# One-core decoder layer with a 32-expert mixture on Trainium2: experts' results written to six places per token and summed at the end

## The chip, the core and the metric

The kernel runs on one core of one Trainium2 chip. The metric is device time in microseconds (us). Before the change the median of three runs is 601.46 us (599.84 to 603.62). One further execution was profiled; it took 602.7 us.

## What is computed

2,048 tokens of width 256 (16 sequences of 128, float32) pass three residual sub-layers, each behind a layer norm:

```python
x = x + latent_attention(layernorm(x))     # causal, width 32, rotary
x = x + cross_attention(layernorm(x), ctx) # 32 heads of width 8, 8 key groups, causal
x = x + experts(layernorm(x))              # 32 experts, inner width 96
```

The expert layer decides what the change touches:

```python
probs = softmax(x @ gate.T)                       # 32 per token
top, idx = top_k(probs, 8)
cum = cumsum(top / sum(top))
num_keep = min(sum(cum < 0.8) + 1, 8)             # at least one expert
share = top * (arange(8) < num_keep); share /= sum(share)
out[token] = sum over kept e of share * (silu(g_e(x)) * u_e(x)) @ down_e.T
```

A token can keep up to seven experts, as the seven largest of eight hold at least 7/8 of their sum, more than 0.8. In the data drawn here no token keeps more than six, and 6,801 of the 16,384 token-expert pairs are kept.

## The kernel before

**Blocks and steps.** Everything goes by blocks of P = 128 tokens, one sequence each, B = 16 of them. The instruction order is written out by hand: a loop over steps t (L1063 and after), four steps to a block, issues in each step the score products of a block's cross attention (step, L616: products of keys and queries, a row maximum by VectorE at L656, a second product and the exponential by ScalarE at L661, four score buffers in flight), and squeezes in between pieces of other work, as Python generators that are advanced by one piece per half step: weigh (the product with the values, o_ps, L669), divide, project (L697 to L712, result into xres, which holds all tokens' residual), route, the queries, keys and latent attention of the next group of four blocks, and the early tiles.

**Route** (L714 to L844). For one block or a pair of blocks: layer norm (statistics with one GpSimd operation at L368, the normalisation on VectorE at L373), two transposes (L396), gate product l_ps (L734), the eight largest, exponentials, cumulative sums by three shifted additions (L764), the list of kept experts (kept, L781), a counting product r_ps (L785) with a triangular matrix that ranks each token among those of its expert, the destination rows di (L811), and the shares written into the row tile (L818). Two blocks are routed together, as one set of instructions, except blocks 8, 9 and 12 to 15, which are routed alone: 11 routes. A row has 292 numbers: 256 of data, the token number, and 32 shares. Seven indirect DMAs per block (L825, on GpSimd's queue, the k-th kept expert of every token of the block) scatter the rows to xs in DRAM, one region of 2,048 rows per expert. They are put in a list, waiting, and taken from it two or four to a step.

**Early tiles.** Once the first ten blocks (NEARLY) are counted, expert regions have up to 24 (NF) full tiles of 128 rows whose rows are all sent. These run beside the rest of the attention and behind it, one slot per step at first and two in the last steps and behind them (first_slot, L948 to L985). Tile i passes four slots: its rows are loaded by SP's queue (ext, L935), its two transposes on TensorE (L968) copied by ScalarE (L978); the gate and up product and silu (L167 to L170); a transpose back (L960); the down product with a per-tile weight load ewd (L941 to L944, 96 KB, SP's queue), and the scaling by the share out of the row tile (ScalarE, L984). Then add_rows (L155) issues an accumulating indirect DMA on GpSimd's queue (L157), which adds the tile's 128 result rows of 256 numbers to one of three accumulators acc in DRAM, taken in turn; the index it reads is the column of token numbers in the row tile ext, of which there are six buffers.

**Load of the down weights.** All 32 experts' down weights, 3.1 MB, are loaded by load_down (L846) in four DMAs on SP's queue in step last + 3, when the attention's memory is released.

**Zeros.** From step 4 on SP issues three of a list of bulk DMAs per step: zeros to the padding of xs, zeros to the three accumulators (48 DMAs of 128 KB), then the experts' gate and up weights.

**Late tiles.** After the last block's route the lists of remaining tiles are built from the counts. Then 32 tiles (one per expert, its last rows) and further ones in chunks of four, each under a branch, run one after the other: rows by SP's queue six tiles ahead (L1223), transposes (L1230), copy (L1232), gate and up product (L1239), silu, transpose back (L1256), down product (L1269), share (L1273) and add_rows. In this data there are 23 full early tiles and 52 late ones, the rounding to four included. For an expert's last tile a predicated copy on VectorE (L1261) masks the token numbers of rows that another tile has.

**The sum at the end** (L1323 to L1340). For two blocks at a time SP loads the three accumulators' rows (24 DMAs of 256 KB), VectorE adds them to xres (L1333, L1335), and the output goes out on ScalarE's queue.

## Time and profile before

| | us |
|---|---|
| median of three runs | 601.46 |
| profiled execution | 602.7 |
| its span in the profile | 600.8 |
| granted TensorE clock, mean | 0.869 |
| attention and what runs beside it, until about | 357 |
| early tiles behind the attention, until the first late row load | 459 |
| late tiles and the landing of their last result, until | 572 |
| sum at the end | 29 |

| engine | busy us | share of the span |
|---|---|---|
| TensorE (PE) | 454.9 | 76% |
| VectorE (DVE) | 350.2 | 58% |
| GpSimd (POOL) | 284.6 | 47% |
| ScalarE (ACT) | 181.0 | 30% |

PE is TensorE's products, PEld its weight loads, which overlap them; SP is the engine whose queue issues most loads. L12 is line 12 of the kernel. In the rows by line, "out<-in" names the destination and the source, "x24" is the number of instructions, then come busy time in us and the mean of one in ns, then the idle time of the engine just ahead of these instructions and what ended it. In the table of waits, "a <- b" says that a waited for b, then the total in us, how often, and the longest. In the rows of the timeline the start and the length in us come first and, in brackets, how long the instruction waited and for what. The share "DMA" is the mean busy share of the core's sixteen DMA engines; GB/s is what they moved. A share over the whole span mixes the stages above.

### The profile page before, as it was taken

The numbers are of one execution on the slowest core, as the hardware profiler recorded it, in microseconds if no ns is written. First come the engines' busy times: TensorE is split into PE (matmuls) and PEld (weight loads), VectorE is DVE, ScalarE is ACT, GpSimd is POOL, SyncE is SP. The second block draws the span as 40 slices with busy tenths as digits, with TensorE's granted clock in tenths as the row PEclk, the third lists the DMA queues.
The fourth block names the chain that finished last, engine by engine and source line by source line (L and its number), as shares of the span: only waits on it lengthen the run. The fifth ranks groups of instructions, "written<-read, shape, count | busy, mean of one in ns | idle before, by whom it ended". The sixth has DMA issues, their size and how long they took to land.

```text
span 600.8 us, 12118 instructions
## 1 busy us (share of the span) xinstructions
PE 454.9 (76%) x4148; PEld 321.1 (53%) x4148; DVE 350.2 (58%) x1222; ACT 181.0 (30%) x450; POOL 284.6 (47%) x292
## 2 busy tenths in 40 slices
PE   4969788986998998988889996445662999988500
PEld 3736475654756665666666655344541666666300
DVE  3464476585676766677757764313440677665456
ACT  1121134333343343523325453112210333332200
POOL 5611230020462473627540478736574688887600
PEclk9978789999899898977889898867775999999955
DMA  8201275705704349301112145864633356567788
GB/s 269 70 1 37 54 172 142 211 1 142 247 28 141 109 123 234 119 16 51 37 35 82 37 94 135 215 149 98 131 58 99 79 103 123 103 107 140 124 272 288
DMA packets 64423, 70.25 MB, mean 117 GB/s; under 512 B 12722, under 2 KB 58808, under 8 KB 64064
## 3 DMA queue, kind: packets, MB, share of 16 engines
q1 hardware_dynamic: 45488, 51.66, 30.3%
q0 software_dynamic: 16320, 14.97, 14.1%
q10 hardware_dynamic: 2544, 2.75, 1.3%
q8 instruction: 35, 0.57, 0.4%
q14 instruction: 36, 0.29, 0.2%
HBM read 38.97 MB, written 42.13 MB: 135 GB/s over the span
## 4 chain that ended last, share of the span: by engine, by line
PE 43%; DVE 21%; DMA 18%; issue 6%; ACT 6%; POOL 3%; SPq 1%; POOLq 0%; DVEq 0%; ACTq 0%
PE s_ps L636 6%; DMA ewd<-in_w_dn_t 5%; DVE nmz L656 4%; PE o_ps L669 4%; PE s_ps L642 4%; DMA part<-acc 4%; DMA acc<-y,xt 4%; ACT xT L1232 2%; PE h_ps L1256 2%; PE q_ps L578 2%; PE s_ps L649 2%; DMA q<-qd 2%; PE egx_ps L968 2%; DVE ga L169 2%; DVE h L170 2%
## 5 line engine op out<-in xcount | busy, mean ns | idle before, releaser
L825 POOL DMA_INDIRECT xs<-row,di x112 | 110.8, 990 | 36.8 <-issue 30.2
L656 DVE TENSOR_REDUCE nmz<-s_ps 128x4 f32<-128x512 f32 x128 | 82.4, 686 | 61.1 <-PE s_ps L649 58.2
L661 ACT ACTIVATE pt<-s_ps 128x512 f32<-128x512 f32 x128 | 69.5, 595 | 104.1 <-PE s_ps L649 99.8
L636 PE MATMUL s_ps<-k,q 32*128 32x128 f32 x1024 | 88.2, 307 | 0.5 <-DVE xres L506 0.5
L642 PE MATMUL s_ps<-q8m,k 32*128 32x512 f32 x256 | 79.7, 709 | 5.5 <-DVE q8m L611 2.6
L636 PEld LDWEIGHTS s_ps<-k,q 32*128 32x128 f32 x1024 | 74.9, 207 | 3.5 <-issue 1.8
L157 POOL DMA_INDIRECT acc<-y,slot x32 | 49.4, 1542 | 19.9 <-DVE y L1273 10.4
L1239 PE MATMUL g<-wgu,xT 128*128 128x192 f32 (+1 forms) x212 | 53.3, 335 | 3.8 <-issue 3.8
L157 POOL DMA_INDIRECT acc<-ey,ext x24 | 37.8, 1575 | 26.3 <-ACT ey L984 17.4
L1232 ACT COPY xT<-x_ps 128x256 f32<-128x256 f32 x55 | 20.5, 372 | 87.2 <-PE x_ps L1230 67.3
L958 PE MATMUL eyh_ps<-ewd,ehT 96*128 96x256 f32 x48 | 19.6, 497 | 33.2 <-DMA ewd<-in_w_dn_t 31.8
L1239 PEld LDWEIGHTS g<-wgu,xT 128*128 128x128 f32 x212 | 36.8, 196 | 8.1 <-ACT th L167 4.5
L669 PE MATMUL o_ps<-pt,va 128*32 128x512 f32 x256 | 38.1, 670 | 1.9 <-DVE xres L712 1.9
L642 PEld LDWEIGHTS s_ps<-q8m,k 32*128 32x128 f32 x256 | 22.1, 203 | 30.4 <-issue 19.5
L169 DVE SCALAR_TENSOR_TENSOR ga<-th,g 128x96 f32<-128x96 f32 x53 | 13.5, 254 | 41.1 <-ACT th L167 27.4
L1269 PE MATMUL y_ps<-wdn,hT 96*128 96x256 f32 (+1 forms) x104 | 35.9, 427 | 0.1
L157 POOL DMA_INDIRECT acc<-y,xt x20 | 30.8, 1542 | 9.6 <-DVE hT L1258 6.9
L675 ACT ACTIVATE ot<-o_ps,tab 128x512 f32<-128x512 f32 x32 | 22.1, 690 | 31.4 <-PE o_ps L669 27.6
L1230 PE MATMUL x_ps<-tab,xt 128*128 128x128 f32 x110 | 22.1, 285 | 11.4 <-DMA xt<-xs 11.3
L958 PEld LDWEIGHTS eyh_ps<-ewd,ehT 96*128 96x128 f32 x48 | 9.4, 232 | 37.0 <-issue 31.2
L368 POOL TENSOR_TENSOR rs_f<-ve_f,mhalf 128x1 f32<-128x1 f32 (+1 forms) x11 | 7.5, 686 | 44.6 <-DVE ve_f L366 44.6
L978 ACT COPY exT<-egx_ps 128x256 f32<-128x256 f32 x24 | 8.9, 373 | 64.0 <-PE egx_ps L968 64.0
(261 smaller groups left out, 884.6 us busy)
## 6 DMA issues: line engine op xcount, KB each, us to landing
xt<-xs SPq DMA_DIRECT2D x58, 146.0 KB
acc<-zero SPq DMA_DIRECT2D x48, 128.0 KB
wgu<-in_w_gu_t SPq DMA_DIRECT2D x32, 192.0 KB
part<-acc SPq DMA_DIRECT2D x24, 256.0 KB
xs<-zero SPq DMA_DIRECT2D x33, 146.0 KB
ext<-xs SPq DMA_DIRECT2D x24, 146.0 KB
ewd<-in_w_dn_t SPq DMA_DIRECT2D x24, 96.0 KB
ct<-in_ctx_t SPq DMA_DIRECT2D x4, 512.0 KB
```

Source lines behind the costliest of these rows:

```text
L157: nc.gpsimd.indirect_dma_start(out=acc[i % NACC], out_offset=bass.IndirectOffsetOnAxis(ap=tokens, axis=0), in_=y, in_offset=None, bounds_c ...
L169: nc.vector.scalar_tensor_tensor(a, th, 1.0, g, ALU.add, ALU.mult)
L636: nc.tensor.matmul(s_ps[:, i, :], lhsT=q8[g % 2][rows, i, tok], rhs=k8[g % 2][h][rows, tok], start=(i == 0), stop=True, skip_group_check=True,
L642: nc.tensor.matmul(s_ps, lhsT=k8[g % 2][h][rows, tok], rhs=q8ms[b][rows, :, :], start=True, stop=True, skip_group_check=True,)
L656: nc.vector.tensor_reduce(nmz[b % 2][:, :, 32 * r + h], s_ps, AX.X, ALU.max, negate=True)
L661: nc.scalar.activation(pt, s_ps, AF.Exp)
L669: nc.tensor.matmul(o_ps[32 * r : 32 * r + 32, :, :], lhsT=vaug[b % NVA][:, 4 * h + r, :], rhs=pts.pop((b, h, r)), start=True, stop=True,)
L825: sent = nc.gpsimd.indirect_dma_start(out=xs, out_offset=bass.IndirectOffsetOnAxis(ap=di[:, j, k : k + 1], axis=0), in_=row[:, j, :], in_o ...
L958: nc.tensor.matmul(y_ps, lhsT=down["hT"], rhs=down["wd"], start=True, stop=True)
L1232: nc.scalar.copy(v["xT"], x_ps)
L1239: nc.tensor.matmul(v["g"], lhsT=v["xT"][:, c, :], rhs=wgu_flat[:, bass.ds(v["e"] * W2 + c * NE * W2, W2)], start=(c == 0), stop=(c == KC - 1),
L1269: nc.tensor.matmul(y_ps, lhsT=hT, rhs=wdn[:, bass.ds(v["e"] * D, D)], start=True, stop=True)
```

## The change

It has five parts.

1. **Places.** A DRAM buffer ys has six rows per token and a section with one more row per token for a seventh. Each result row is written to a place of its own by a plain indirect DMA, with no order among these DMAs; an index beyond the buffer is dropped. The place of a token's result for an expert is six times the token number plus the number of its kept experts ahead of this one, a prefix sum over 32 columns: nine more VectorE operations in each route, with a running maximum that tells whether any token keeps a seventh. Row tiles are 320 wide: 256 of data and 32 pairs of share and place. In an early tile's slot ScalarE copies the pair out of the row tile and VectorE turns the place into an index; in a late tile one VectorE operation does so, masked where it is an expert's last tile. The row tiles of early tiles have five buffers instead of six. Zeros are written to all of ys (16 DMAs of 768 KB and 4 of 512 KB) in place of the accumulators.
2. **The sum at the end** loads one block's 128 x 6 rows with one DMA (768 KB, 6 KB contiguous per partition, eight buffers in the memory of the gate and up weights); VectorE adds the first half to the second and GpSimd two of the three rows that are left, VectorE adds the third and GpSimd's sum to the residual; an output DMA follows per block. A branch ahead of it adds the seventh section if a token has one.
3. **Routes.** All blocks are routed alone, 16 routes; the list of waiting sends is kept by blocks, and its thresholds change with it.
4. **Counting later.** While the attention runs, the counting product is issued half a step later; the prefix sum and what follows it stand in a further piece of the generator.
5. **The down weights' four DMAs** are issued on ScalarE's queue.

```diff
-RW = 292
-R_TOK, R_SHARE = D, D + 1
+RW = D + 2 * NE
+R_PAIR = D
+KEPT = 6
+NOWHERE = 16384
...
+    ys = dram.tile([(KEPT + 1) * B * P, D], F32, tag="ys", name="ys")
...
-    def add_rows(i, y, tokens):
-        nc.gpsimd.indirect_dma_start(
-            out=acc[i % NACC],
-            out_offset=bass.IndirectOffsetOnAxis(ap=tokens, axis=0),
-            in_=y, in_offset=None, bounds_check=B * P - 1, oob_is_err=False,
-            compute_op=ALU.add,
+    def place_rows(y, place):
+        sent = nc.gpsimd.indirect_dma_start(
+            out=ys, out_offset=bass.IndirectOffsetOnAxis(ap=place, axis=0),
+            in_=y, in_offset=None, bounds_check=(KEPT + 1) * B * P - 1, oob_is_err=False,
         )
+        tc.declare_no_dep(sent.ins, group="placed", reason="places are distinct")
+        tc.add_to_no_dep_group("placed", sent.ins)
...
-            g, pair = b0, b0 // 2
-            if b0 % 2 == 0:
-                while waiting and waiting[0][0] < pair - 2:
-                    waiting.pop(0)[1]()
-                rows[pair] = work.tile([P, 2, RW], F32, tag="row", bufs=3, name=f"row_{g}")
-                nc.gpsimd.memset(rows[pair][:, :, R_SHARE + NE :], 0.0)
-                nc.gpsimd.tensor_copy(
-                    rows[pair][:, :, R_TOK].bitcast(I32), num[:, b0 : b0 + 2]
-                )
-            row = rows[pair][:, b0 % 2 : b0 % 2 + nb, :]
+            g = b0
+            while waiting and waiting[0][0] < b0 - 3:
+                waiting.pop(0)[1]()
+            row = work.tile([P, nb, RW], F32, tag="row", bufs=4, name=f"row_{g}")
+            pairs = row[:, :, R_PAIR:].rearrange("p j (e i) -> p j e i", i=2)
...
+            nc.vector.tensor_tensor(seventh, seventh, act[:, 0, 6:7], ALU.max)
...
             yield
+            if dense[0]:
+                yield
             r_ps = mm([P, nb, NE], f"r_ps_{g}")
...
+            yield
+            pre = [t[:, 0:nb, :] for t in pres]
+            nc.vector.tensor_copy(pre[0][:, :, 17:], kept[:, :, 0 : NE - 1])
+            for k in range(5):
+                c, d = pre[k % 2], 1 << k
+                nc.vector.tensor_tensor(
+                    pre[1 - k % 2][:, :, 16:], c[:, :, 16:], c[:, :, 16 - d : 16 - d + NE], ALU.add
+                )
+            nc.vector.tensor_scalar(
+                pre[0][:, 0, 16:], pre[1][:, 0, 16:], float(KEPT),
+                tab[:, C_SEVENTH + b0 : C_SEVENTH + b0 + 1], ALU.is_ge, ALU.mult,
+            )
+            nc.vector.scalar_tensor_tensor(
+                pairs[:, 0, :, 1], pre[1][:, 0, 16:], tab[:, C_PLACE + b0 : C_PLACE + b0 + 1],
+                pre[0][:, 0, 16:], ALU.add, ALU.add,
+            )
             nc.vector.tensor_tensor(kept, kept, ex[:, :, 0:NE], ALU.mult)
             sk = small.tile([P, nb], F32, tag="sk", name=f"sk_{g}")
...
-                row[:, :, R_SHARE : R_SHARE + NE], kept, 0.5,
+                pairs[:, :, :, 0], kept, 0.5,
...
-                    waiting.append((pair, lambda j=j, k=k: send(j, k)))
+                    waiting.append((b0, lambda j=j, k=k: send(j, k)))
...
-                nc.sync.dma_start(
+                nc.scalar.dma_start(
...
-        bulk += [(a[b * P : (b + 1) * P, :], zero[:, 0:D]) for a in acc for b in range(B)]
+        for b in range(B):
+            r = b * P * KEPT
+            bulk.append(
+                (
+                    ys[r : r + P * KEPT, :].rearrange("(p k) d -> p k d", k=KEPT),
+                    zero[:, 0:D].unsqueeze(1).to_broadcast([P, KEPT, D]),
+                )
+            )
...
+        for b in range(0, B, 4):
+            r = (KEPT * B + b) * P
+            bulk.append(
+                (
+                    ys[r : r + 4 * P, :].rearrange("(k p) d -> p k d", p=P),
+                    zero[:, 0:D].unsqueeze(1).to_broadcast([P, 4, D]),
+                )
+            )
...
-        alone = (NEARLY - 2, NEARLY - 1, *range(B - 4, B))
-        routed = {b: (b - 1, 2) for b in range(1, B, 2)}
-        routed.update({b: (b, 1) for b in alone})
+        waiting, turn, count, counted = [], [0], [0], []
+        routed = {b: (b, 1) for b in range(B)}
...
-            v["xt"] = ebuf.tile([P, RW], F32, tag="ext", bufs=SOON + 4, name=f"ext_{k}")
+            v["xt"] = ebuf.tile([P, RW], F32, tag="ext", bufs=SOON + 3, name=f"ext_{k}")
...
+                pair = ebuf.tile([P, 2], F32, tag="epair", bufs=5, name=f"epair_{i}")
+                nc.scalar.copy(pair, turn_["xt"][:, bass.ds(2 * e_act + R_PAIR, 2)])
+                turn_["place"] = ebuf.tile([P, 1], I32, tag="eplace", bufs=6, name=f"eplace_{i}")
+                nc.vector.tensor_scalar(
+                    turn_["place"], pair[:, 1:2], float(NOWHERE), None, ALU.add
+                )
+                turn_["share"] = pair[:, 0:1]
...
-                nc.scalar.mul(y, y_ps, down["xt"][:, bass.ds(e_act + R_SHARE, 1)])
-                add_rows(i - 3, y, down["xt"][:, R_TOK : R_TOK + 1].bitcast(I32))
+                nc.scalar.mul(y, y_ps, down["share"])
+                place_rows(y, down["place"])
...
-            if t >= last or waiting and 4 * NEARLY < t and waiting[0][0] < NEARLY // 2:
+            if t >= last or waiting and 4 * NEARLY < t and waiting[0][0] < NEARLY:
...
+        pair = v["xt"][:, bass.ds(2 * e_dve + R_PAIR, 2)]
+        place = hbuf.tile([P, 1], I32, tag="place", bufs=4, name=f"place_{i}")
         if i < NE:
-            nc.vector.copy_predicated(slot[:, i : i + 1], valid[:, i : i + 1], tokens)
-            tokens = slot[:, i : i + 1]
+            nc.vector.tensor_scalar(
+                place, pair[:, 1:2], valid[:, i : i + 1], float(NOWHERE), ALU.mult, ALU.add
+            )
+        else:
+            nc.vector.tensor_scalar(place, pair[:, 1:2], float(NOWHERE), None, ALU.add)
...
-        nc.vector.tensor_scalar(
-            y, y_ps, v["xt"][:, bass.ds(e_dve + R_SHARE, 1)], None, ALU.mult
-        )
-        add_rows(NF + i, y, tokens)
+        nc.vector.tensor_scalar(y, y_ps, pair[:, 0:1], None, ALU.mult)
+        place_rows(y, place)
...
-    PB = 2
-    for b in range(0, B, PB):
-        part = hbuf.tile([P, NACC, PB, D], F32, tag="part", bufs=3, name=f"part_{b}")
-        for k in range(NACC):
-            nc.sync.dma_start(
-                out=part[:, k, :, :],
-                in_=acc[k][b * P : (b + PB) * P, :].rearrange("(b p) d -> p b d", p=P),
-            )
-        xg = xres[:, b : b + PB, :]
-        for k in range(NACC - 1):
-            nc.vector.tensor_tensor(xg, xg, part[:, k, :, :], ALU.add)
-        for j in range(PB):
-            nc.vector.scalar_tensor_tensor(
-                xg[:, j, :], xg[:, j, :], some[:, b + j : b + j + 1], part[:, NACC - 1, j, :],
-                ALU.mult, ALU.add,
-            )
-        nc.scalar.dma_start(
-            out=out[b * P : (b + PB) * P, :].rearrange("(b p) d -> p b d", p=P), in_=xg
+    with tc.If(nc.values_load(sevenths[0:1, 0:1], min_val=0, max_val=B * P) > 0):
+        for b in range(B):
+            part = hbuf.tile([P, D], F32, tag="part7", bufs=2, name=f"part7_{b}")
+            r = (KEPT * B + b) * P
+            nc.sync.dma_start(out=part, in_=ys[r : r + P, :])
+            nc.vector.tensor_tensor(xres[:, b, :], xres[:, b, :], part, ALU.add)
+    parts = wgu_flat.rearrange("p (n k d) -> p n k d", n=8, d=D)
+    for b in range(B):
+        part = parts[:, b % 8, :, :]
+        nc.sync.dma_start(
+            out=part,
+            in_=ys[b * P * KEPT : (b + 1) * P * KEPT, :].rearrange("(p k) d -> p k d", k=KEPT),
         )
+        half = hbuf.tile([P, KEPT // 2, D], F32, tag="half", bufs=3, name=f"half_{b}")
+        nc.vector.tensor_tensor(half, part[:, 0:3, :], part[:, 3:6, :], ALU.add)
+        both_b = hbuf.tile([P, D], F32, tag="both", name=f"both_{b}")
+        nc.gpsimd.tensor_tensor(both_b, half[:, 0, :], half[:, 1, :], ALU.add)
+        xb = xres[:, b, :]
+        nc.vector.scalar_tensor_tensor(
+            xb, xb, some[:, b : b + 1], half[:, 2, :], ALU.mult, ALU.add
+        )
+        nc.vector.tensor_tensor(xb, xb, both_b, ALU.add)
+        nc.scalar.dma_start(out=out[b * P : (b + 1) * P, :], in_=xb)
```

## The prediction

> **What bounds the kernel now.** I read the span in stretches first, then who waits for whom in each stretch, then single instructions. The table of stretches (start:end, length, busy time of each engine, granted TensorE clock, DMA share, GB/s):
>
> ```profile
> core 0: us, PE busy (x) PEld busy (x) DVE busy (x) ACT busy (x) POOL busy (x), PEclk, DMA share, GB/s
> 250.00:357.00 107.00, 94.73 (x1148) 67.85 (x1146) 74.28 (x283) 43.57 (x96) 49.70 (x59) 0.87 0.18 50
> 357.00:442.00 85.00, 49.66 (x250) 37.91 (x246) 30.79 (x154) 21.80 (x69) 54.46 (x49) 0.78 0.61 135
> 442.00:459.00 17.00, 5.15 (x26) 3.89 (x26) 4.93 (x26) 0.45 (x1) 12.80 (x12) 0.52 0.24 47
> 459.00:572.00 113.00, 93.94 (x478) 67.54 (x478) 66.78 (x242) 33.80 (x108) 80.20 (x52) 0.95 0.60 114
> 572.00:601.00 29.00, 0.00 (x0) 0.00 (x0) 17.74 (x32) 0.00 (x0) 0.00 (x0) 0.50 0.86 290
> ```
>
> Four regimes. Up to 357 us TensorE is nearly full. From 357 to 459 no compute engine is: 102 us for 20 slots of early tiles. From 459 the 52 late tiles run one after the other, TensorE bound. The last 29 us are transfer alone, 6.29 MB of sums in and 2.10 MB out. The waits inside 357 to 460 (waiter <- awaited: us in total, times, longest), of TensorE and then of SP's queue:
>
> ```profile
> PE eyh_ps L958 <- DMA ewd<-in_w_dn_t: 31.8, 8, 14.5
> ...
> SPq L935 <- DMA acc<-ey,ext: 55.1, 13, 13.6
> SPq L1223 <- DMA xs<-row,di: 12.6, 1, 12.6
> ```
>
> TensorE stands 31.8 us for weights of an early tile; SP stands 55.1 us at the row load ahead of them in its order (L935), because the row buffer is still read by an accumulating DMA: its token numbers are the index. The 14.5 is one wait, where that weight load lies behind the four down-weight loads of 379 us. Then SP waits 12.6 us for GpSimd's last sends.
>
> **The change, part by part**, against the profiled execution's 602.7 us.
>
> Places instead of sums. GpSimd's price today, per DMA:
>
> ```profile
> L825 POOL DMA_INDIRECT xs<-row,di x112 | 110.8, 990 | 36.8 <-issue 30.2 <-DVE row L818 3.0 <-DVE xn_a L373 1.1
> ...
> L157 POOL DMA_INDIRECT acc<-ey,ext x24 | 37.8, 1575 | 26.3 <-ACT ey L984 17.4 <-ACT xnt_f L400 3.6 <-issue 2.5
> ```
>
> A plain scatter takes 0.99 us, an accumulating one 1.57; back to back each adds 0.30 of idle. A place is a plain scatter of 1,024 B rows, so between 0.97 and 1.57; I take 0.99, the row of the same kind. From the first early result on, GpSimd has 40 sends and 24 results today: 40 x 1.29 + 24 x 1.87 = 96.5 us. In the built order of the change it has 31 sends and 24 places there, since blocks routed alone hand over their sends earlier: 55 x 1.29 = 71 us. The place and share are copied out of the row tile (one ScalarE copy, one VectorE operation per early tile), so the load at L935 no longer waits for a result to land.
>
> From 357 to 459 us. Of the 31.8, I keep 5 for the down weights, which still move 3.1 MB through the same sixteen engines while row and weight loads go on: -26.8. ScalarE issues the four down-weight loads, 1.8 us on SP today, and 24 small copies: +2. SP's 12.6 shrinks to what the last block's own sends need: its last counting product (L785) is followed by about 4.5 us of VectorE and 9 scatters of 1.3, 16 us, where today the last send starts 20.4 after it (436.7 to 457.2): -4. Together some **-28**. The counting starts a step later, so one slot of 2.9 us (neighbours start at 409.86 and 412.76) moves behind that product, where TensorE and the late lists end after 13 us and the sends after 18: it is hidden there, and 2 us fall out of the attention. Bounds of the 28: -35 if the weights cost nothing beside the rest and the sends wait for nothing, -13 if the 14.5 stay and half of the 4 is won. Late next: VectorE's and ScalarE's part of a slot, or GpSimd's 71 us, which from 346 end no earlier than 417; my 431 for the first late row load lies behind both.
>
> Here a rule speaks against the change. The wait of 14.5 us began when SP had issued 3.1 MB just ahead. The Trainium skill, "DMA: Bandwidth & Descriptors", "Issuing engines are not separate DMA queues", says that a second issuing engine saves issue time alone, as all transfers run on the same engines. By it the sum would be 9.5 higher, 604.0. The same page, "Queues, rings and completion order", lets each engine take turns between queues packet by packet, which a load behind others in one queue has not; no row of this trace shows the two queues busy with loads together.
>
> Routing alone, prefix sums, counting later (up to 357 us). TensorE's first score products of a step show the pace. Block 8's route, alone, falls into 272.7 to 289.6, 16.9 us for a block. One pair's route falls into the two blocks from 222.8 to 255.1, 16.1 each with 1.8 of key and value products: 14.3 without. So a lone route costs up to 2.6 us more per block. Ten blocks lose their partner; the first six lie before 250 us, where TensorE is 88 to 90% busy and has the next groups' products to do meanwhile, so I let half show there: 6 x 1.3 + 4 x 2.6 = +18. The counting product (L785) waits today:
>
> ```profile
> 279.29 0.64 PE L785 MATMUL r_ps<-kept,tab 128*128 128x32 f32 x2 [1.41 <-DVE kept L781]
> ...
> 280.29 1.94 PE L669 MATMUL o_ps<-pt,va 128*32 128x512 f32 x8
> ```
>
> After the wait the product L669 takes 1.94 us; without one, at 270.93, 1.07. Moved behind that product, the count waits some 0.5 and the product runs at 1.07: -1.7 for each of the 14 blocks routed before 357 us, -24. Against that stand nine more VectorE operations per block at a spacing of 0.2 (L764 takes 0.175), 1.8 us. They are queued ahead of the next block's normalisation (L373), for which TensorE's transposes (L396) wait: in the lone block's rows TensorE could take these at some 285.2 at the new pace, while VectorE, after the score reductions (1.3), the nine and the shares (2.4) and the normalisation (0.6), is there at 286.8. So the 1.7 is lost again; half in the eight blocks with cover, 8 x 0.9 + 6 x 1.8 = +18. Together 18 - 24 + 18 = **+12**, and **-2** for the slot that leaves. Bounds of the 12: -6 with the nine hidden, +27 with all of the split's 26 and all of the nine's 25 shown.
>
> Zeros and wider rows. 14.7 MB of zeros instead of 6.3 is 23 us of all engines at the 362 GB/s seen from 584 to 597, in a stretch (107 to 250) with shares of 0.40 and 0.59, so about 74 us free. The queue's next reader, the third group's queries, has 60 us until its first step. **0**, bound +3. Rows of 1,280 for 1,168 B: within that.
>
> Late tiles. From the first transpose to the last result, 465.7 to 565.2, 52 tiles take 99.5 us; at the steady 1.83 they would take 95.2. The surplus holds the stall from 545.7 to 553.9, a row load that waits 5.42 us for an accumulating DMA. It goes; GpSimd's 1.85 per tile falls to 1.3, but TensorE stays at 1.83. **-3**, from -4.3 to +3.4, the latter if 20 added operations of 0.17 were all exposed; VectorE is 59% busy here, which hides them.
>
> Last landing and branch. Issue to first sum load is 5.7 us today (566.4 to 572.1); a plain scatter is issued in 0.99 and lands in a median of 2.7 after its issue: -2. The branch over the seventh place, not taken unless a token keeps seven, costs every engine a load and a jump: +1. **-1**, from -2 to +2.
>
> The sum at the end. 12.58 MB in and 2.10 out, 14.68 for 8.39. Packets of 1,024 B have a median of 46 ns and of 4,096 B 159 ns, 22.3 and 25.8 B/ns on each of 16 engines; a place row is 6,144 B. Two measured stretches bound it:
>
> ```profile
> 382.00:396.00 14.00, 1.30 (x10) 1.04 (x8) 1.47 (x6) 1.15 (x4) 8.93 (x11) 0.72 1.04 268
> 584.00:597.00 13.00, 0.00 (x0) 0.00 (x0) 10.52 (x19) 0.00 (x0) 0.00 (x0) 0.50 1.04 362
> ```
>
> The first is the down weights in rows of up to 10,240 B, the second today's sums. At 362 GB/s the stage grows from 23.2 to 40.6, +17.4; with loads at 268 and outputs at 362 to 52.7, +29.5; at the 412 that 25.8 B/ns would be, to 35.6, +12.4. I take 385, between the rates of 1 and 4 KB: 38.1, **+15**. VectorE's three additions a block (1.0 + 0.48 + 0.4 by the 0.69 and 0.48 of L1333 and L1335) and GpSimd's one (0.7, a quarter of 2.36 and some fixed part) fit in the 2.4 that a block's bytes take.
>
> The Trainium skill, "SBUF — State Buffer", "Who interferes with whom", says that VectorE with two SBUF inputs and GpSimd reading SBUF block each other. No row shows that here; run one after the other, the same rows give an estimate of 2.6 for the 2.4 of a block and put the sum 3 higher.
>
> Sum: 12 - 2 - 28 + 0 - 3 - 1 + 15 = -7, so 595.7 for an execution like the profiled one. That one lies 1.2 above the median of 601.46; **594.5** beside the median.
>
> **Rivals.** First, the place rows load slowly. Large rows ran at 268 GB/s in the one stretch that has them; against it, that source has rows 32 KB apart on 96 partitions, and places are contiguous. Price 29.5 - 15 = 14.5: **609**, slower than before. The sign turns where the last stage grows by over 22, and 1% is passed below some 277 GB/s of loads.
>
> Second, VectorE becomes the bound of the attention. For it: 74.3 of 107 us busy already, and four score buffers tie it to TensorE; against it, up to 250 us there is cover. With all of split and nine shown, +27 for +12: **609.5**. It decides where a block's VectorE work passes TensorE's, both 15 to 17 us by the rows above.
>
> Third, the stretch behind the attention doesn't shrink as told: the second queue does nothing for the weights, or the row load meets another late reader. -13 for -28: **609.5**.
>
> Fourth, the nine operations hide wholly, -6 for +12: **576.5**.
>
> **Chances.** The forecast 0.50, its own range 586 to 602; slow rows 0.13; VectorE 0.15; the small shrink 0.10; all hidden 0.12. About 1% (6 us) is what a measurement can tell from none. Of the forecast's half, 0.32 lies below 595.4; with the hidden case, faster 0.44. The slow cases scatter round 609, and two of them together go beyond 620: of their 0.38, 0.30 lies above 607.5, with 0.02 of the forecast slower 0.32; same 0.24. With a tenth left out at either end: 577 to 616.
>
> **What would show it.** Right: TensorE's wait for early weights falls from 31.8 to under 10 us, SP's for an early result's landing is gone, the first late row load lies 15 to 30 us nearer to the last score product, GpSimd's places take 0.99, late tiles stay at 1.83, and the last stage takes some 44 us at about 385 GB/s. Wrong: a block of attention over 18.5 us with VectorE without idle time; a rate of the last stage below 330 GB/s; a wait of over 10 us behind the down weights.

## The result and the profile after

The change makes the kernel slower: 653.49 us (median of 4 runs, 647.14 to 659.46) for 601.52, a ratio of 1.079 (95% interval 1.073 to 1.086). The ratio compares the fast executions alone, without the one of 659.46. The prediction was 594.5, at most 616. The profiled execution took 654.26 us, its span 652.5 for 600.8.

Where the time went, from the first and last instructions of the stages in the two profiles (us):

| stage | before | after | difference | predicted |
|---|---|---|---|---|
| start to the last score product | 357.9 | 408.4 | +50.5 | +10 |
| from there to the first late row load | 101.3 | 81.7 | -19.6 | -28 |
| late tiles, to the issue of the last result | 107.1 | 106.5 | -0.6 | -3 |
| to the first load of the sum | 5.8 | 5.4 | -0.4 | -1 |
| sum at the end | 28.7 | 50.5 | +21.8 | +15 |

The table of stretches of the changed kernel (the columns are those of the prediction's first table):

```profile
core 0: us, PE busy (x) PEld busy (x) DVE busy (x) ACT busy (x) POOL busy (x), PEclk, DMA share, GB/s
300.00:408.40 108.40, 88.17 (x998) 61.64 (x998) 79.17 (x333) 39.74 (x93) 40.82 (x47) 0.84 0.17 54
408.40:490.10 81.70, 54.82 (x283) 41.00 (x279) 43.34 (x233) 24.44 (x87) 49.96 (x52) 0.79 0.47 145
490.10:602.00 111.90, 94.50 (x478) 68.50 (x478) 67.74 (x262) 33.80 (x108) 50.60 (x52) 0.94 0.41 122
602.00:652.50 50.50, 0.00 (x0) 0.00 (x0) 30.79 (x48) 0.00 (x0) 14.37 (x16) 0.50 0.73 291
```

Two things are to be seen: in the last line the DMA share is 0.73, where it was 0.86 before, so transfers no longer set the end; and the attention runs at a granted clock of 0.84.

**The attention.** The same steps, from 100 us to the last score product, before:

```profile
100.00:357.90 257.90, 228.98 (x2818) 157.93 (x2816) 175.47 (x602) 104.62 (x225) 105.95 (x126) 0.92 0.34 99
```

and after:

```profile
100.00:408.40 308.40, 248.50 (x2805) 172.60 (x2803) 217.04 (x831) 106.03 (x236) 108.09 (x121) 0.83 0.36 115
```

TensorE does the same products in 248.5 us that took 229.0: +19.5, at a clock of 0.83 for 0.92. The rest of the 50.5, 31 us, is idle time of TensorE (59.9 for 28.9), and VectorE ends almost all of it: its waits for VectorE sum to 58.3 us, for 27.0 before. The longest entries in the waits of TensorE before, from 100 to 357.9 us:

```profile
PE r_ps L785 <- DVE kept L781: 11.6, 7, 1.9
PE some_ps L349 <- DVE m L347: 4.8, 1, 4.8
```

and after, from 100 to 408.4 us, with the counting product's entry last:

```profile
PE o_ps L678 <- DVE xres L721: 13.4, 9, 2.9
PE tp_f L405 <- DVE row L382: 10.6, 7, 1.8
PE q_ps L587 <- DVE xnt_b L411: 8.4, 2, 5.3
PE c_ps L424 <- DVE xnt_a L411: 5.5, 1, 5.5
...
PE r_ps L792 <- DVE kept L786: 0.9, 1, 0.9
```

The counting product, 11.6 us of waits before, is down to 0.9. Others have taken its place: products whose input VectorE makes behind the route's operations. One such place in the timeline, in the order of the rows' start:

```profile
160.43 0.59 PE L651 MATMUL s_ps<-q8m,k 32*128 32x512 f32 x2
...
161.80 2.85 DVE L818 TENSOR_SCALAR di<-d 128x8 int32<-128x8 f32 x1
162.26 2.36 POOL L420 TENSOR_TENSOR xres<-xres,bres 128x1024 f32<-128x1024 f32 x1
...
165.97 1.09 DVE L826 TENSOR_TENSOR pre<-pre 128x32 f32<-128x32 f32 x5
...
168.61 0.68 DVE L411 COPY xnt_a<-tp_a 128x512 f32<-128x512 f32 x1
169.35 3.20 PE L424 MATMUL c_ps<-wcc,xnt_a 128*128 128x32 f32 x14 [5.45 <-DVE xnt_a L411]
172.47 1.22 PE L651 MATMUL s_ps<-q8m,k 32*128 32x512 f32 x2
...
173.49 1.06 PE L651 MATMUL s_ps<-q8m,k 32*128 32x512 f32 x2
```

TensorE needs the copy L411 of the next group's latent attention from 163.9 us on. VectorE reaches it at 168.6, behind an index operation that took 2.85 instead of its median 0.17 while GpSimd's 2.36 ran, behind two score maxima, behind the prefix sum and behind the next normalisation. TensorE stands for 5.45 us. Then it runs at half clock: the two pairs of score products L651 take 1.22 and 1.06 us, for 0.70 and 0.59 at 160 us. The table of stretches gives the clock:

```profile
152.00:164.00 12.00, 8.73 (x102) 6.36 (x102) 9.23 (x33) 3.34 (x6) 6.77 (x7) 0.72 0.88 218
164.00:166.00 2.00, 0.00 (x0) 0.00 (x0) 1.97 (x5) 0.00 (x0) 0.61 (x1) 0.96 1.06 363
166.00:176.00 10.00, 6.65 (x56) 5.54 (x60) 4.45 (x17) 1.02 (x3) 1.96 (x2) 0.50 1.03 348
```

So one late copy costs 5.5 us of waiting and about half of TensorE's 6.65 us in the 10 us at half clock, which begin some 2 us into the wait. The Trainium skill, "TensorE: Matmul & The Clock Gate", "HAM oscillation — how this bites in real kernels", warns of idle gaps of TensorE beyond some 3.4 us. The wait of 5.45 us agrees with that, but here shorter waits were enough, and the measurement decides:

```profile
183.70 0.58 PE L444 MATMUL qk_ps<-cht,wbd 128*128 128x128 f32 x1 [2.86 <-DVE cht L440]
```

```profile
183.00:189.00 6.00, 5.30 (x48) 4.65 (x49) 3.93 (x13) 0.63 (x2) 0.62 (x1) 0.50 0.86 312
```

By the trace's clock records TensorE spends 102 us from 100 to 408.4 us at half clock, for 41 from 100 to 357.9 before. Each of the 16 stretches of half clock begins during a wait for VectorE of 1.1 to 5.5 us or within 2 us of its end; not every wait of that length has one (3.07 us at 137 has none). The prediction had priced VectorE's operations at VectorE's own time and had left the clock out.

**The stretch behind the attention.** The waits of TensorE and of SP's queue from 408 to 491 us, the longest of TensorE and those of SP that answer to the rows of before:

```profile
PE eyh_ps L996 <- DVE eh L174: 6.4, 7, 3.2
...
SPq L1267 <- DMA xs<-row,di: 7.4, 1, 7.4
SPq L971 <- DMA ewd<-in_w_dn_t: 4.1, 1, 4.1
```

The 31.8 us of waits for early weights are gone, and so are SP's 55.1 for an accumulating DMA; the wait for the last sends is 7.4 us, for 12.6. The table leaves out SP's waits for buffers of early weights (L980, 33.6 us); TensorE's list has no wait for these weights.

**The sum at the end.** The steady state of one block, from the timeline of the changed kernel:

```profile
640.34 0.95 DVE L1385 TENSOR_TENSOR half<-wgu 128x768 f32<-128x768 f32 x1
641.33 0.48 DVE L1389 SCALAR_TENSOR_TENSOR xres<-xres,some,half 128x256 f32<-128x256 f32 x1
641.43 0.96 POOL L1387 TENSOR_TENSOR both<-half 128x256 f32<-128x256 f32 x1 [1.47 <-DVE half L1385]
642.43 0.43 DVE L1392 TENSOR_TENSOR xres<-xres,both 128x256 f32<-128x256 f32 x1 [0.62 <-POOL both L1387]
```

A block takes 2.43 us, 16 of them 39.2 (606.1 to 645.3); the loads are all issued at 630, at 416 to 420 GB/s. GpSimd's addition takes 0.96 us beside VectorE's 0.48, and in the first four blocks, where it began together with L1389, 0.72, and L1389 took 1.05. Either way the two are done some 1.05 us after the first of them began.

### The profile page after: what moved, and what is told of

The parts are those of the page before. It is cut to its first block, busy times and chain, and to the rows that moved or that the text cites. A ratio compares the mean times of both kernels' runs of the same rounds, so it can differ in the third digit from the quotient of the medians.

```text
span 652.5 us, 12579 instructions
## 1 busy us (share of the span) xinstructions
PE 476.2 (73%) x4160; PEld 336.0 (51%) x4160; DVE 413.9 (63%) x1542; ACT 185.9 (28%) x484; POOL 254.9 (39%) x298
## 4 chain that ended last, share of the span: by engine, by line
PE 35%; DVE 31%; issue 13%; POOL 11%; DMA 6%; ACT 2%; POOLq 1%; SPq 0%; DVEq 0%; ACTq 0%
POOL ys L160 8%; DVE nmz L665 6%; PE s_ps L645 5%; PE o_ps L678 4%; PE s_ps L651 3%; DVE pre L826 2%; PE q_ps L587 2%; DVE half L1385 2%; DMA ys<-y,place 2%; PE s_ps L658 2%; POOL both L1387 2%; PE egx_ps L1004 2%; PE v_ps L550 2%; DVE q8m L620 1%; PE c_ps L424 1%
## 5 line engine op out<-in xcount | busy, mean ns | idle before, releaser
L645 PE MATMUL s_ps<-k,q 32*128 32x128 f32 x1024 | 91.9, 322 | 0.5 <-DVE xres L515 0.5
L651 PE MATMUL s_ps<-q8m,k 32*128 32x512 f32 x256 | 86.2, 761 | 5.1 <-DVE s L759 2.1
L645 PEld LDWEIGHTS s_ps<-k,q 32*128 32x128 f32 x1024 | 78.2, 221 | 3.2 <-issue 1.8
L160 POOL DMA_INDIRECT ys<-y,place x52 | 50.6, 973 | 58.2 <-DVE y L1321 58.2
L678 PE MATMUL o_ps<-pt,va 128*32 128x512 f32 x256 | 40.7, 713 | 13.4 <-DVE xres L721 13.4
L377 POOL TENSOR_TENSOR rs_f<-ve_f,mhalf 128x1 f32<-128x1 f32 x16 | 9.6, 599 | 83.2 <-DVE ve_f L375 46.6
L160 POOL DMA_INDIRECT ys<-ey,eplace x24 | 23.6, 982 | 28.3 <-ACT ey L1027 11.5
L651 PEld LDWEIGHTS s_ps<-q8m,k 32*128 32x128 f32 x256 | 23.2, 214 | 19.3 <-issue 11.5
L684 ACT ACTIVATE ot<-o_ps,tab 128x512 f32<-128x512 f32 x32 | 22.0, 688 | 35.2 <-PE o_ps L678 33.6
L1387 POOL TENSOR_TENSOR both<-half 128x256 f32<-128x256 f32 x16 | 14.4, 898 | 32.9 <-DVE half L1385 32.9
L994 PE MATMUL eyh_ps<-ewd,ehT 96*128 96x256 f32 x48 | 18.6, 474 | 10.7 <-issue 5.2
L1321 DVE TENSOR_SCALAR y<-y_ps,xt 128x256 f32<-128x256 f32 x52 | 24.8, 477 | 0.0
L587 PE MATMUL q_ps<-xnt_b,xwq 128*128 128x512 f32 x32 | 17.7, 681 | 8.4 <-DVE xnt_b L411 8.4
```

What stands on the lines that cost most here:

```text
L160: sent = nc.gpsimd.indirect_dma_start(out=ys, out_offset=bass.IndirectOffsetOnAxis(ap=place, axis=0), in_=y, in_offset=None, bounds_check= ...
L587: nc.tensor.matmul(q_ps, lhsT=xwq[:, c, h * P : (h + 1) * P], rhs=xnt[:, c, :], start=(c == 0), stop=(c == KC - 1),)
L645: nc.tensor.matmul(s_ps[:, i, :], lhsT=q8[g % 2][rows, i, tok], rhs=k8[g % 2][h][rows, tok], start=(i == 0), stop=True, skip_group_check=True,
L651: nc.tensor.matmul(s_ps, lhsT=k8[g % 2][h][rows, tok], rhs=q8ms[b][rows, :, :], start=True, stop=True, skip_group_check=True,)
L678: nc.tensor.matmul(o_ps[32 * r : 32 * r + 32, :, :], lhsT=vaug[b % NVA][:, 4 * h + r, :], rhs=pts.pop((b, h, r)), start=True, stop=True,)
L1321: nc.vector.tensor_scalar(y, y_ps, pair[:, 0:1], None, ALU.mult)
```

## The experiments

The kernel before takes 602 us where it was first measured and 603 on one other chip, and 668 to 673 on three more, where TensorE stands 0.2 to 2.5 us ahead of single score products for no reason that the profile shows. Every ratio below is to the kernel before on the same chip; stage lengths are compared among chips of one kind, called below chips of 602 us and chips of 670 us.

| run | ratio to the kernel before (95%) | last score product, us | to the first late row load | sum at the end |
|---|---|---|---|---|
| *chips of 668 to 673 us* | | | | |
| kernel before, one execution | 1.00 | 427.5 | 103.9 | 28.2 |
| changed kernel again | 1.065 (1.061 to 1.070) | 453.7 | 94.0 | 50.5 |
| split only | 1.012 (1.006 to 1.017) | | | |
| nine more only | 1.012 (1.003 to 1.021) | 421.5 | 104.5 | 28.1 |
| later count only | 1.001 (0.996 to 1.005) | 416.6 | 104.5 | 29.0 |
| split and nine | 1.038 (1.030 to 1.046) | 449.4 | 102.4 | 28.3 |
| split, nine, later count | 1.027 (1.021 to 1.033) | 444.1 | 102.2 | 28.3 |
| changed, no prefix | 1.014 (1.007 to 1.020) | 432.4 | 87.7 | 50.7 |
| changed, no prefix, early count | 1.012 (1.002 to 1.023) | | | |
| changed, early count | 1.032 (1.027 to 1.038) | 442.5 | 93.1 | 50.5 |
| changed, prefix on GpSimd | 1.023 (1.014 to 1.031) | 428.3 | 93.5 | 50.4 |
| changed, last addition written a block later | 1.058 (1.051 to 1.066) | 456.4 | 92.3 | 50.3 |
| changed, sum on VectorE alone | 1.055 (1.050 to 1.061) | 454.0 | 92.4 | 42.3 |
| down weights on ScalarE's queue only | 1.002 (0.998 to 1.006) | 412.1 | 104.9 | 28.2 |
| row tile copied only | 0.974 (0.970 to 0.977) | | | |
| row tile copied, down weights on ScalarE | 0.981 (0.968 to 0.994) | | | |
| *a chip of 603 us* | | | | |
| prefix on GpSimd, sum on VectorE | 1.023 (1.014 to 1.031) | 368.0 | 87.9 | 42.4 |
| row tile copied, again | 0.979 (0.974 to 0.984) | 359.2 | 88.6 | 28.4 |

(Empty where the profiled execution is not comparable. The kernel before and two of its small variants put the last score product at 412 to 428 us on chips of 670 us, so differences of under 10 us in that column say little.)

### The parts of the attention, one at a time, in the kernel before

All blocks routed alone:

```diff
-        alone = (NEARLY - 2, NEARLY - 1, *range(B - 4, B))
-        routed = {b: (b - 1, 2) for b in range(1, B, 2)}
-        routed.update({b: (b, 1) for b in alone})
+        routed = {b: (b, 1) for b in range(B)}
```

> The kernel before with every block routed alone (16 routes for 11), nothing else changed. In the changed kernel the last score product ended 50.6 us later (408.4 for 357.8), and TensorE spent 102 us at half clock in the attention for 41. Theory A (VectorE's longer order delays TensorE, stalls of some us lower the granted clock, and the two add up): the split alone costs 15 to 30 us, the last score product lies at 373 to 388, the half-clock time rises by 20 us or more. Theory B (counting later is what costs): the split costs under 5 us.

Nine more operations per route: the running maximum, then a copy, five additions and two more, on tiles that the route has done with:

```diff
+            pre = [left[:, :, 0:NE], lw[:, :, 0:NE]]
+            nc.vector.tensor_copy(pre[0], kept)
+            for k in range(5):
+                nc.vector.tensor_tensor(pre[1 - k % 2], pre[k % 2], kept, ALU.add)
...
```

> The kernel before with nine more VectorE operations in each of its 11 routes, at the places where the change has them; their results are not used. 11 x 9 x about 0.2 = some 20 us of VectorE. Theory A: 10 to 25 us slower, with the last score product at 368 to 383. My prediction's best rival (all nine hidden): within 3 us of the kernel before. Theory B: within 5 us.

The later count:

```diff
             yield
+            if dense[0]:
+                yield
             r_ps = mm([P, nb, NE], f"r_ps_{g}")
```

> The kernel before with only the counting product issued half a step later while the attention runs. My prediction priced this step at -24 us for 14 blocks routed alone; by the same step some 7 waits of 11.6 us in all go here, so -10 to -20. Theory A: -12 to 0, since VectorE's order gets no longer. Theory B: 15 us slower or more.

Measured: +1.2%, +1.2% and nothing, 8, 8 and 0 us. The split costs less than theory A said, the nine slightly less, and the later count gains none of my 10 to 20 us, though the waits of the counting product go (0.5 us are left). Theory B falls for this context. Then two of them together, and all three (the later count for blocks 0 to 7):

> The kernel before with all blocks routed alone and the nine more VectorE operations in each of the 16 routes, counting as early as before. Alone the split gave a ratio of 1.012, the nine 1.012. If they add up, with nine operations in 16 routes for 11: 1.025 to 1.03, last score product 16 to 20 us later. If they act together as in the changed kernel: 1.04 or more.

> The same with the counts of blocks 0 to 7 issued half a step later. In the changed kernel the early count of these blocks was worth 19 us. If the later count costs wherever VectorE's order is long: 10 to 20 us slower than the split with nine and early counts. If it costs only with what else the change does (sends and rows in another order): within 5 us of it.

Split and nine cost 3.8%, 25 us: above the 1.025 to 1.03 of a sum and near the 1.04 of acting together, though the intervals of the two parts (up to 1.017 and 1.021) leave room for a plain sum. The later count does not add to them; if anything it takes 1% off (the two intervals overlap). So whatever it costs in the changed kernel depends on something else there.

### The same parts taken out of the changed kernel

Without the prefix sum (each expert has a place of its own, so that one operation writes them; the sum at the end leaves out the results of experts 6 to 31):

```diff
-            nc.vector.tensor_copy(pre[0][:, :, 17:], kept[:, :, 0 : NE - 1])
...
+            nc.vector.tensor_scalar(
+                pairs[:, 0, :, 1], tab[:, C_IOTA : C_IOTA + NE],
+                tab[:, C_PLACE + b0 : C_PLACE + b0 + 1], None, ALU.add,
+            )
```

> The changed kernel with 32 places for each token (one per expert), so that a place is a table's number and the prefix sum goes: one VectorE operation per route in place of nine. It leaves out of the sum at the end the results of experts 6 to 31; bytes loaded and written as zeros are the same. Theory A: the last score product comes 12 to 25 us earlier than 408.4, time 628 to 641. Theory B: under 5 us earlier.

With the later count for blocks 8 and after alone (`if dense[0] and b0 >= 8`), and with both edits:

> The changed kernel with the counting product of blocks 0 to 7 issued as early as in the kernel before. Theory A: the later count shortens no VectorE work and only moves it, so the time changes by under 6 us either way. My prediction's step (counting later saves 1.7 us per block): 8 x 1.7 = 14 us slower.

> The changed kernel without the prefix sum (32 places per token, results of experts 6 to 31 left out of the sum) and with the counts of blocks 0 to 7 as early as before. Without the prefix alone the ratio to before was 1.0136, with the early count alone 1.0323, the change itself 1.0654. If both are separate costs: 0.98 to 0.99. If the later count costs only because the prefix lies behind it: 1.005 to 1.02.

With the changed kernel run beside the kernel before on a chip of this kind:

> The changed kernel once more, beside the kernel before on one chip. In the last four runs the kernel before took 667.8 us in place of 601.5, and TensorE stood for single instructions in its score products. Theory A (the change's own work in the attention costs 50 us through VectorE and the granted clock): 45 to 58 us slower than the kernel before wherever it runs. Theory C (the attention's pace has two levels, and the chip decides as much as the kernel): where the kernel before takes 600 us the change is 45 to 58 us slower, where it takes some 667 us the change is within 20 us of it, since the attention's loss is there already.

The change costs 6.5% there, 43 us: theory C falls, though the attention loses 26 us (427.5 to 453.7), half of what it lost on the first chip, and theory A's 45 to 58 us is narrowly missed too. There the kernel before runs its attention at a clock of 0.83 already, in its own profile:

> The kernel before, unchanged, for a profile on a chip of the experiments. Theory A (a stall of TensorE costs twice, as wait and as lower granted clock): where it takes some 670 us, the early part, the late tiles and the sum at the end last as before (107 and 29 us), the whole surplus of some 60 us lies in the attention, with a granted clock of about 0.82 there in place of 0.92 and waits of TensorE that VectorE and ScalarE don't explain.

```profile
100.00:427.50 327.50, 261.58 (x2855) 178.47 (x2847) 176.44 (x604) 106.08 (x227) 105.32 (x126) 0.83 0.27 79
```

261.6 us of products, for 229.0 on the first chip, so most of the part of the loss that comes from the clock is there before the change adds anything; the changed kernel has 267.9 there, at 0.81.

The ladder in ratios: 1.065 for the change, 1.032 with the early count, 1.014 without the prefix, 1.012 without both. Without the prefix the count's place makes no difference; with it the later count costs 3%. In TensorE's waits, of the early count first and of the change on the same chip second:

```profile
PE r_ps L792 <- DVE kept L786: 12.5, 7, 3.3
PE s_ps L651 <- DVE s L759: 7.3, 5, 3.2
...
PE tp_f L405 <- DVE row L382: 5.0, 3, 1.8
```

```profile
PE s_ps L651 <- DVE s L759: 13.3, 6, 4.7
PE tp_f L405 <- DVE row L382: 10.6, 6, 1.8
PE o_ps L678 <- DVE xres L721: 8.4, 6, 2.9
PE q_ps L587 <- DVE xnt_b L411: 7.8, 2, 4.8
```

The 12.5 us at the counting product go (1.3 are left), and more than that comes back in other products: TensorE's waits for VectorE are 49.8 us with the early count and 69.5 with the change.

### The prefix sum on another engine

The decisive edit moves the work and removes none (the product of kept and exponentials goes to another tile, so that VectorE doesn't wait for GpSimd):

```diff
-            nc.vector.tensor_copy(pre[0][:, :, 17:], kept[:, :, 0 : NE - 1])
+            nc.gpsimd.tensor_copy(pre[0][:, :, 17:], kept[:, :, 0 : NE - 1])
...
-                nc.vector.tensor_tensor(
+                nc.gpsimd.tensor_tensor(
...
```

> The changed kernel with the prefix sum (eight of the nine operations, ten instructions there) on GpSimd in place of VectorE. Theory A (VectorE's order is what delays TensorE): 10 to 25 us faster than the changed kernel. Rival (GpSimd's operations hold the memory port that VectorE needs, or delay the statistic that the next normalisation waits for): no gain, or slower than the changed kernel by up to 15 us.

29 us faster than the change (1.0654 to 1.0225), a little beyond theory A's range; the last score product is back at 428. The rival falls here: GpSimd does ten operations of 0.2 to 0.42 us per route with no loss that shows.

### The sum at the end

```diff
+    for b in range(B + 1):
...
+        if b >= 1:
+            xb = xres[:, b - 1, :]
+            nc.vector.tensor_tensor(xb, xb, boths.pop(b - 1), ALU.add)
```

> The changed kernel with VectorE's last addition and the output of each block issued one block later at the end. In the changed kernel a block takes 2.43 us there (16 blocks from 606.1 to 645.3) in a chain of VectorE 0.95, GpSimd 0.96, VectorE 0.42. If the chain's latency is the cause, a block takes 1.9 to 2.1 us, and the last stage shrinks from 50.5 to 43 to 46 us. If VectorE and GpSimd block each other (VectorE's L1389 took 1.05 beside GpSimd's operation and 0.48 without), a block stays at 2.3 to 2.6 and the stage at 49 to 53.

```diff
-        nc.gpsimd.tensor_tensor(both_b, half[:, 0, :], half[:, 1, :], ALU.add)
+        nc.vector.tensor_tensor(both_b, half[:, 0, :], half[:, 1, :], ALU.add)
```

> The changed kernel with GpSimd's addition at the end on VectorE: four VectorE operations per block, no GpSimd. With the port theory a block takes the sum of the four (0.95 + 0.48 + two of 0.34 to 0.48), 2.1 to 2.3 us, and the last stage falls from 50.5 to 46 to 48; if GpSimd's part was hidden, VectorE's longer order makes a block 2.5 or more, and the stage 51 to 53.

The first edit did not reach the order on the chip. In its profile each block's last addition (L1396) still stands ahead of the next block's L1387 and waits for its own block's GpSimd addition; here are the first block's and the start of the second:

```profile
664.68 1.01 POOL L1389 TENSOR_TENSOR both<-half 128x256 f32<-128x256 f32 x1 [9.11 <-DVE half L1387]
665.73 0.42 DVE L1396 TENSOR_TENSOR xres<-xres,both 128x256 f32<-128x256 f32 x1 [0.61 <-POOL both L1389]
666.07 0.95 DVE L1387 TENSOR_TENSOR half<-wgu 128x768 f32<-128x768 f32 x1
```

So its 2.43 us per block and 50.3 for the stage are those of the changed kernel once more and decide nothing between the two readings; what a truly later addition would win stays open. Without GpSimd, from the timeline:

```profile
663.42 0.95 DVE L1385 TENSOR_TENSOR half<-wgu 128x768 f32<-128x768 f32 x1
664.40 0.42 DVE L1387 TENSOR_TENSOR both<-half 128x256 f32<-128x256 f32 x1
...
665.60 0.95 DVE L1385 TENSOR_TENSOR half<-wgu 128x768 f32<-128x768 f32 x1
```

2.18 us per block and 42.3 for the stage, less than the 46 to 48 expected: 4 us are saved in the 16 blocks, and 4 more behind them, since the span ends 7.2 us after the last addition with GpSimd in the loop and 3.1 without. That the two engines hinder each other on these operands is shown by the changed kernel's own rows: L1389 takes 0.48 us, and 1.05 where GpSimd's addition begins with it. The Trainium skill, "SBUF — State Buffer", "Who interferes with whom", says that VectorE with two SBUF inputs and GpSimd reading SBUF block each other; these rows agree with it, where the prediction had let it pass as 3 us.

### The stretch behind the attention

The down weights on the second queue alone, in the kernel before:

```diff
-                nc.sync.dma_start(
+                nc.scalar.dma_start(
                     out=wdn[:, es.start * D : es.stop * D].rearrange("p (e d) -> p e d", d=D),
```

> The kernel before with the down weights' four DMAs on ScalarE's queue, nothing else. If the second queue frees the early tiles' weights: the longest wait of TensorE for them (14.5 us) falls under 5, and the stretch from the last score product to the first late row load is 8 to 14 us shorter than its 101 to 104. If transfers share the engines whichever queue issues them, or SP's wait for the accumulating DMA decides: within 4 us.

Nothing (1.002). TensorE's and SP's waits are those of the kernel before, the 14.5 us a 14.8:

```profile
PE eyh_ps L958 <- DMA ewd<-in_w_dn_t: 28.7, 6, 14.8
```

```profile
SPq L935 <- DMA acc<-ey,ext: 55.7, 14, 11.2
```

So the rule of the Trainium skill that the prediction weighed against the change ("DMA: Bandwidth & Descriptors", "Issuing engines are not separate DMA queues") gives the right answer for this part. This run alone does not prove it, since SP's 55.7 us of waits at the row load remain in it; the same edit without them follows below. Then the row tile alone:

```diff
+                turn_["tok"] = ebuf.tile([P, 1], I32, tag="etok", bufs=6, name=f"etok_{i}")
+                nc.vector.tensor_copy(
+                    turn_["tok"], turn_["xt"][:, R_TOK : R_TOK + 1].bitcast(I32)
+                )
...
+                nc.scalar.copy(turn_["share"], turn_["xt"][:, bass.ds(e_act + R_SHARE, 1)])
...
-                add_rows(i - 3, y, down["xt"][:, R_TOK : R_TOK + 1].bitcast(I32))
...
+                add_rows(i - 3, y, down["tok"])
```

> The kernel before with an early tile's token numbers and share copied out of its row tile (one VectorE and one ScalarE operation per early tile, five row buffers for six), so that SP's row load no longer waits for an accumulating DMA; all else, the accumulators too, as before. My step: SP's 55.1 us of waits go and most of TensorE's 31.8, so the stretch from the last score product to the first late row load falls from 101 by 12 to 20 us. Rival: the down weights ahead of the tile's weights in SP's queue still cost their 14.5, and GpSimd's 96.5 us of sends and accumulations take over as the bound: 0 to 8 us.

> The kernel before with the token numbers and share copied out of the row tile, and the down weights on ScalarE's queue. With the copy alone the ratio to the kernel before was 0.9735. If the second queue is worth what the prediction thought (a wait of 14.5 us behind the down weights): 0.955 to 0.965. If the release of the row tile was the whole of it, as TensorE's missing waits for early weights with the copy alone say: 0.968 to 0.979.

> The kernel before with the token numbers and share copied out of the row tile, once more: 0.970 to 0.980 if the first measurement holds; within 0.99 to 1.0 if the gain lay within the spread of the attention from run to run.

0.974, and 0.979 on another chip: 590.6 us for 602.9, faster than both kernels. With the second queue too it is 0.981 (0.968 to 0.994), no gain that can be told. In the stretch behind the attention the waits of TensorE for early weights, 31.8 us before, are gone, with the down weights on SP's queue and the accumulators as they were; what ends most of TensorE's waits now is VectorE, and SP's first late row load waits for GpSimd's last sends:

```profile
PE eyh_ps L960 <- DVE eh L170: 9.7, 5, 6.9
PE tp_f L396 <- DVE row L373: 5.7, 1, 5.7
```

```profile
SPq L1227 <- DMA xs<-row,di: 12.6, 1, 12.6
```

So GpSimd's order of sends and accumulations, which I had thought the next bound, is what ends the stretch of 88.6 us: from 361.25 to 446.74 its 34 sends and 19 accumulations follow each other with the usual 0.3 us between them and only 6.5 us of idle time beside, and the first late row load is issued 1.1 us behind the last of them.

### What is left of the change without its two faults

The prefix on GpSimd and the sum on VectorE, together:

> The changed kernel with the prefix sum on GpSimd and the whole sum at the end on VectorE. The prefix on GpSimd alone gave 1.0225, VectorE's sum shortened the last stage by 8.2 us (1.2%). If these are separate: 1.007 to 1.015, that is, what is left is the larger sum at the end (42 for 28 us) less the 10 us won behind the attention. If the places win more than that: below 1.0.

1.023 on a chip of 602 us, where the change itself had 1.079: 613.5 us. The stretch table from 100 us to its last score product:

```profile
100.00:368.00 268.00, 228.55 (x2833) 157.22 (x2828) 195.13 (x735) 107.18 (x241) 139.97 (x233) 0.92 0.42 133
```

The clock is back at 0.92, TensorE's products at 228.6 us, its waits for VectorE at 37.1. Of the attention's 50.5 us the prefix's place on VectorE had cost 40. The spans differ by 8.3: attention +10.1, the stretch behind it -13.4, sum +13.7, the rest -2. 1.023 is above the 1.007 to 1.015 I expected (its interval begins at 1.014). The sum and the stretch came out much as expected; the attention's 10.1 us, for which the expectation had left nothing, make the difference, and which part of the change they belong to is open. The stretch wins 13.4 there, not the change's 19.6: SP's first late row load waits 10.7 us for GpSimd's last sends, for 7.4 in the change, and GpSimd does the last route's prefix sum (438.5 to 441.7) ahead of some of these; how much of the 6.2 us that makes was not measured. The places are not worth their larger sum, since the copied row tile brings 12.7 of the 13.4 with the accumulators kept.

## Why the prediction was wrong, point by point

- **Nine operations, "half in the eight blocks with cover, 8 x 0.9 + 6 x 1.8 = +18".** This is the step that failed, together with the next one: the two were added as -24 and +18, as if each had a price of its own. Measured, they depend on each other. With the counts of blocks 0 to 7 early, the nine cost 2.0% (1.012 to 1.032, some 13 us, within the 18); with the count late they cost 5% (1.014 to 1.065, some 35); and both together cost 5.3% (1.012 to 1.065), some 36 us for the predicted -6 (whole times, each ratio on its own chip, with intervals of up to 1% either way). The attention's +50.5 on the first chip lies beyond even the bound of +27. Moving the prefix sum off VectorE gave back 40.4 us of the attention on chips of 602 us (408.4 to 368.0) and 25 to 29 us on one of 670 us. Half of the 40 is TensorE's products at a lower clock (248.5 to 228.6), half waits (58.3 to 37.1). The prediction bounded the price by VectorE's own 25 us, as if a wait cost only its length. Its mechanism was half right: it named TensorE's transposes waiting for VectorE's normalisation behind the nine. Its second rival, VectorE as the bound with no idle time left, is not what happened: VectorE is busy 217.0 of 308.4 us (175.5 of 257.9 before), and TensorE waits for it all the same. The early blocks, which I thought covered, lost most: from 122 us on, the same steps took 137.4 us for 102.0 before.
- **"Moved behind that product, the count waits some 0.5 ... -24".** The wait did go (11.6 to 0.9). No time went with it: by itself the later count is worth nothing in the kernel before, and with the prefix behind it costs 3%, some 22 us for the predicted -24. Why it costs there, and not in the kernel before with split and nine, I haven't settled; the prefix stands in a piece of its own there, and the sends follow in another order.
- **Split, +18.** 8 us alone, and nothing that can be told in the changed kernel without the prefix, whose last score product lies at 432 for 412 to 428.
- **357 to 459 us, -28.** -19.6. The release of the row tile did what was said, and more: none of the 31.8 us of waits for weights is left. Some 11 us come back as waits for VectorE and ScalarE (12.4 and 5.3 us, for 4.4 and 1.8; L996 for L174 is 6.4), which I had named as late next but not priced. The second queue had no part in it.
- **Places at 0.99 us.** Right: the profile's two groups of them have means of 973 and 982 ns.

```profile
L160 POOL DMA_INDIRECT ys<-y,place x52 | 50.6, 973 | 58.2 <-DVE y L1321 58.2
L160 POOL DMA_INDIRECT ys<-ey,eplace x24 | 23.6, 982 | 28.3 <-ACT ey L1027 11.5
```

- **Late tiles -3, landing -1.** -0.6 and -0.4. GpSimd's wait and SP's late row load, which went, had been beside TensorE's work.
- **Zeros, 0.** Not tried by themselves. While they run the DMA share is 0.88 to 1.06, and the repaired kernel, which has them too, is 10 us behind the kernel before at the last score product.
- **The sum at the end, +15.** +21.8. The 16 blocks took 39.2 us for the predicted 38.1, but the size came out right by luck: transfers ran at 416 to 420 GB/s for my 385, at which the bytes take 35 us, and VectorE with GpSimd set the pace at 2.43 us a block. What failed in the mechanism is that their additions "fit in the 2.4 that a block's bytes take": they hinder each other and are the bound. Of the 6.8 us beyond the +15, 5.4 lie at the two ends, which the sum of bytes doesn't hold: 4.1 us until the first load has landed for 2.7 before, and 7.2 behind the last addition for 3.2.

## What to carry to other kernels

Work put on an engine that feeds a nearly full TensorE is priced twice, as waits and as the lower clock behind them; read the granted clock of the stretch before calling anything hidden, and try the work on an engine whose queue nobody waits for. When a load waits for a buffer, look for the small thing that still reads it: two copies of one column each were worth more than a new scheme of places, and more than a second queue. A step that ends one wait of TensorE is worth its length only if the instruction behind it has its inputs.

## What I had not expected of the hardware

- Half clock for some 10 us around one wait of 5.45 us, with products of 1.06 us for 0.59, and half clock again around a wait of only 2.86.
- A VectorE operation of 128 x 8 numbers at 2.85 us, for a median of 0.17, while GpSimd added 128 x 1024 numbers in 2.36.
- The end of the span 7.2 us behind the last addition where GpSimd added in the last stage, and 3.1 where it didn't; the last output has landed some 6 us before the end in the first case (646.6 for 652.5). What GpSimd does in that time the profile doesn't show.
- On three of the chips used the same kernel takes 11% longer, nearly all of it in the attention (69.6 of 71.1 us on the one profiled). TensorE stands there 0.2 to 2.5 us ahead of single products and waits for nothing that the profile names (16 us in all at the score products), and the clock falls to 0.83.
